# An attention and deformable-convolution block on one core: two of five tile transposes go back to TensorE, and all step orders are new

## The chip, the core and the metric

The kernel runs on one core of a Trainium2 chip. The core has five engines, each with its own instruction queue that is worked off strictly in order: TensorE (PE, matrix products; PEld are its weight loads), VectorE (DVE), ScalarE (ACT), GpSimd (POOL) and SyncE (SP, used here to issue DMAs). Engines wait for each other and for DMAs by semaphores. Data lie in SBUF (128 partitions), matmul results in PSUM, the inputs and scratch arrays in DRAM. The metric is the time of one execution in microseconds; the median of three runs counts.

## What is computed

The input x has 4 images of 64 x 64 pixels with 256 channels, in fp32. Two layers follow each other:

```python
# layer 0: attention over the 4096 pixels of each image
q, k, v = x @ wq + bq, x @ wk + bk, x @ wv + bv            # 32, 32, 256 channels
x = gamma * (softmax(q @ k.T) @ v) + x
# layer 1: DCNv3 block
h = ln(x, ln1_g, ln1_b)
x_proj = h @ inproj_w + inproj_b
x1 = gelu(ln(depthwise_conv3x3(h, dw_w) + dw_b, dwln_g, dwln_b))
offset, mask = x1 @ off_w + off_b, softmax(x1 @ mask_w + mask_b)   # 16 groups, 9 points
out = sum over 9 points of mask * bilinear(x_proj at pixel + point + offset)
x = x + out @ outproj_w + outproj_b
x = x + gelu(ln(x, ln2_g, ln2_b) @ fc1_w + fc1_b) @ fc2_w + fc2_b   # 1024 hidden
```

`ln` normalises a pixel over its 256 channels. Such a normalisation wants the pixels on partitions; the convolution and the matmuls that follow want channels on partitions. So tiles of pixels by channels have to be turned, several times for each pixel.

## The kernel before

**Units.** The work is cut into units of 256 pixels (4 image rows): 16 per image, 64 in all. A unit passes these stages: `project` (queries, keys, values), attention (two units together), `front` (normalisation, input projection), `plan` (depthwise convolution, its normalisation, offsets and masks, sampling weights), `sample` (weighted sum of pixels) and `back` (output projection, MLP). The stages `plan`, `sample` and `back` work on 65 units v = 0 to 64 that are shifted by half a unit, as the convolution needs a row of the next one. Units 0 and 64 have one tile of 128 pixels, the others two.

**Order.** Nothing is ordered by data alone. Each stage is a dictionary of named steps. `whole` (its function is at the end of the kernel) gives each step of each unit a number, sorts all steps by it and emits the instructions in that order; each engine's queue gets its share of this one sequence. The number is `slot * T + WHEN[stage][name]` with T = 120. A slot holds two units, "a" and "b", so the pattern repeats 32 times; `LATE` replaces the numbers in slots at the ends and around a change of image. T is no time: the numbers of `WHEN` lie on a grid of 120/337, that is, they are positions in an order of 337 places per slot. A wait arises where an instruction stands in its queue before what it needs is there.

**Turning a tile.** There are two ways. `transposed` (line 347) makes TensorE transpose 128 x 128 pieces against an identity matrix, four for a tile of 256 x 256, into a PSUM buffer. The other way goes through DRAM: `sent` (line 290) stores the tile to a scratch array `ways`, `blocks` (line 285) loads it back with four DMAs that put its 32 x 32 blocks into their turned places (`in_blocks`, line 70, in runs of 32 numbers, which are 128 bytes), and `swapped` (line 295) turns the insides of the blocks with one VectorE stream transpose of 128 x 512. Before the change five tiles of a unit go through DRAM: the normalised input of `front` (`bl_f`), the convolution of `plan` (`bl_c`), its normalised form (`bl_p`), the sampled sum in `back` (`bl_s`, from `spd`) and the normalised tile before the MLP (`bl_b`). Query, key and value inputs of images 1 to 3 are also loaded in blocks. The first unit and the last ones use TensorE: in `plan` the flag `through` is true for units 1 to 57.

**The steps of `plan` that matter here.** `tap0` (ScalarE) and `tap1` to `tap8` (VectorE) form the convolution `cv`, channels on partitions. `send` stores it (SP queue), `turn` issues the four block loads (SP queue), `swap` makes `pc` with pixels on partitions. `stats` takes mean and variance of pc's rows (VectorE) and starts 1/sqrt on GpSimd, `shift` (VectorE) and `norm` (ScalarE) give `xn`, which `norm` also stores (ScalarE's DMA queue). `turn2` issues four loads again (SP), `swap2` makes `ge`, `gelu` (ScalarE) applies scale, bias and GELU in place. `heads0` and `heads1` (TensorE, 432 columns) give offsets and masks, `bias0` and `bias1` (VectorE) add the biases, and the steps that follow, on VectorE and ScalarE, make sampling weights of them.

**Buffers.** All small products in PSUM (the heads, the hidden layer `ph` in eight pieces, the narrowed `pm`, and those of project, front and back) share the pool tag "m" with two buffers that are taken in turn: the third waits until the first is released. Attention has PSUM buffers of its own (`e0`, `e1`, `acc0`, `acc1`). In SBUF, `xs` (two buffers) holds what `blocks` loads and `cT` (four buffers) the turned tiles; `cv` and `xn` have one buffer each.

Of the kernel before, what the change touches and what calls it, by code (L numbers as in the profile page):

```python
# [20 lines left out]
def tile_attention_dcnv3_block(  # L21
# [23 lines left out]
    nc = tc.nc  # L45
# [301 lines left out]
    def transposed(src, name, n=2, pool=None, tag="m"):  # L347

        pt = (pool or ps).tile([P, C // P, 256], F32, tag=tag, name=f"pt_{name}")
        for k in range(C // P):  # L350
# [19 lines left out]
            "turn": 19.72, "load": 37.2107, "copy": 73.8872, "values": 84.2136, "value_copy": 94.184,  # L370
            "keys": 147.9525, "key_bias": 149.3769,
        },
        "projectb": {
            "turn": 79.72, "load": 112.7003, "copy": 119.822, "values": 126.9436, "keys": 127.6558,
            "value_copy": 130.1484, "key_bias": 132.2849,
        },
        "tablesa": {
            "gelu0": 64.6291, "gelu1": 68.9021, "exp": 84.9258,
        },
        "tablesb": {  # L380
            "gelu0": 158.9911, "gelu1": 170.0297, "exp": 179.2878,
        },
        "fronta": {
            "inverse": -50.3858, "residual": -46.8249, "stats": -45.7567, "shift": -39.7033, "norm": -30.8012,
            "turn": -27.2404, "swap": -12.2849, "scale": -10.1484, "project_in": -5.1632, "image": -4.8071,
            "keep": -4.451, "store": -0.5341, "add": 1.6024,
        },
        "frontb": {
            "inverse": -42.1958, "residual": -41.8398, "stats": -21.8991, "shift": -5.8754, "norm": -0.8902,
            "keep": 9.4362, "turn": 15.1335, "swap": 22.9674, "scale": 27.2404, "image": 29.7329,  # L390
            "project_in": 78.8724, "store": 82.4332, "add": 86.7062,
        },
        "plana": {
            "tap0": -4.095, "tap1": -1.9585, "tap2": 6.2315, "tap3": 8.0119, "tap4": 11.9288, "tap5": 14.7774,
            "tap6": 16.5579, "tap7": 18.3383, "tap8": 19.0504, "send": 23.3234, "turn": 25.1039,
            "carry": 28.3086, "swap": 35.0742, "stats": 37.5668, "shift": 41.8398, "norm": 47.8932,
            "turn2": 51.8101, "swap2": 62.4926, "gelu": 66.4095, "heads0": 70.3264, "bias0": 70.6825,
            "heads1": 71.3947, "bias1": 77.092, "mask_exp": 81.365, "hat0": 82.0772, "hat1": 82.7893,
            "sums": 83.5015, "hat2": 86.3501, "nearer": 87.0623, "invert": 87.4184, "weigh": 89.5549,
            "near": 89.911, "mask": 90.9792, "product0": 92.4036, "y0": 93.1157, "y_copies0": 94.5401,  # L400
            "product1": 95.2522, "y_copies1": 95.9644, "y1": 97.0326, "x_copies": 97.3887, "bounds": 100.5935,
            "x": 101.6617, "count": 105.5786,
        },
        "planb": {
            "tap0": 30.8012, "tap1": 34.7181, "tap2": 38.2789, "tap3": 40.4154, "tap4": 40.7715,
            "tap5": 41.4837, "tap6": 43.6202, "tap7": 45.4006, "tap8": 53.5905, "send": 61.4243,
            "turn": 62.8487, "swap": 68.546, "stats": 69.9703, "shift": 74.5994, "norm": 79.5846,
            "turn2": 88.4866, "carry": 90.6231, "swap2": 98.8131, "gelu": 101.3056, "heads0": 104.1543,
            "heads1": 104.5104, "bias0": 108.0712, "bias1": 108.7834, "mask_exp": 110.2077, "sums": 114.4807,
            "hat0": 116.9733, "hat2": 120.178, "invert": 122.6706, "hat1": 124.095, "nearer": 125.8754,  # L410
            "weigh": 127.2997, "near": 129.0801, "mask": 131.5727, "product0": 140.4748, "y0": 144.3917,
            "y_copies0": 150.4451, "product1": 151.1573, "y_copies1": 152.5816, "y1": 153.2938,
            "x_copies": 153.6499, "x": 156.4985, "count": 186.7656, "bounds": 198.5163,
        },
        "samplea": {
            "rows03": 6.5875, "rows04": 80.6528, "rows14": 83.8576, "rows00": 103.4418, "times00": 103.4421,
            "rows01": 105.9344, "times01": 105.9347, "plus01": 106.2908, "rows02": 106.6466,
            "times02": 106.6469, "times03": 107.003, "plus02": 108.4273, "plus03": 112.3442,
            "times04": 116.6172, "rows12": 117.3291, "times12": 117.3294, "plus04": 118.7537,
            "across00": 122.3145, "rows11": 123.0264, "times11": 123.0267, "across01": 123.3828,  # L420
            "rows13": 128.368, "across02": 133.7092, "rows10": 134.065, "times10": 134.0653,
            "plus11": 136.2018, "plus12": 136.9139, "times13": 141.1869, "times14": 141.543,
            "plus13": 142.6113, "plus14": 143.6795, "across10": 148.6647, "across11": 151.5134,
            "across12": 154.0059,
        },
        "sampleb": {
            "rows04": 135.8457, "rows01": 160.059, "times01": 160.0593, "rows03": 162.1958, "rows02": 162.5516,
            "times02": 162.5519, "rows00": 163.2638, "times00": 163.2641, "plus01": 165.7567,
            "plus02": 168.6053, "times03": 171.454, "plus03": 173.2344, "times04": 176.4392,
            "plus04": 177.5074, "rows13": 178.2196, "across00": 180.0, "across01": 181.7804,  # L430
            "rows11": 183.9166, "times11": 183.9169, "across02": 184.9852, "rows10": 185.3409,
            "times10": 185.3412, "rows12": 186.0531, "times12": 186.0534, "plus11": 187.8338,
            "plus12": 188.1899, "rows14": 191.7507, "times13": 194.9555, "times14": 196.0237,
            "plus13": 201.0089, "plus14": 205.2819, "across10": 211.6914, "across11": 213.4718,
            "across12": 219.1691,
        },
        "backa": {
            "turn": 163.9763, "copy": 166.8249, "load": 171.0979, "project_out": 175.727, "added": 178.9318,
            "stats": 181.0682, "shift": 187.4777, "norm": 192.819, "turn2": 205.638, "swap": 205.9941,
            "scale": 208.1306, "hidden0": 213.8279, "gelu0": 214.8961, "hidden1": 216.6766, "gelu1": 217.7448,  # L440
            "hidden2": 218.457, "gelu2": 220.9496, "hidden4": 222.3739, "hidden6": 222.73, "gelu4": 223.0861,
            "gelu6": 223.7982, "raised": 251.2166, "hidden7": 255.4896, "hidden3": 257.27, "gelu7": 259.4065,
            "gelu3": 259.7626, "hidden5": 264.0356, "gelu5": 264.7478, "narrowed0": 269.0208,
            "narrowed1": 272.2255, "end": 275.7864,
        },
        "backb": {
            "turn": 219.8813, "copy": 230.5638, "load": 233.7685, "project_out": 237.6855, "added": 241.2463,
            "stats": 243.7389, "shift": 250.5045, "norm": 252.6409, "turn2": 260.8309, "swap": 266.5282,
            "raised": 267.5964, "scale": 272.9377, "hidden0": 279.7033, "hidden2": 281.1276, "gelu0": 282.908,
            "hidden7": 284.3323, "gelu2": 284.6884, "hidden5": 286.4688, "gelu7": 287.181, "hidden1": 287.5371,  # L450
            "gelu1": 288.9614, "gelu5": 289.3175, "hidden4": 290.3858, "gelu4": 290.7418, "hidden3": 292.1662,
            "hidden6": 294.3027, "gelu3": 295.0148, "gelu6": 295.3709, "narrowed0": 297.8635,
            "narrowed1": 298.5757, "end": 307.1217,
# [30 lines left out]
        },  # L484
        "attentiona": {
            "load": -59.6439, "k0": -59.2878, "k1": -57.8635, "e0": -55.727, "x0": -48.9614, "e3": -47.8932,
            "x3": -46.4688, "e1": -44.6884, "k2": -44.3323, "x1": -43.2641, "e2": -42.5519, "wa0": -40.7715,
            "x2": -40.0593, "wa1": -38.2789, "e5": -36.8546, "wb0": -35.4303, "k3": -32.2255, "wa2": -29.7329,
            "wb1": -28.6647, "x5": -27.9525, "wb2": -24.3917, "wa3": -23.6795, "e4": -20.4748, "k4": -19.7626,
            "wb3": -17.9822, "x4": -15.1335, "e7": -12.6409, "wb4": -10.8605, "x7": -10.5045, "e6": -8.724,  # L490
            "wa4": -8.0119, "wb5": -6.9436, "x6": -6.5875, "k6": -3.7389, "e9": -1.6024, "wb6": 0.5341,
            "wa5": 0.8902, "x9": 1.9585, "wa6": 4.451, "e8": 4.8071, "x8": 5.5193, "wa7": 8.724, "k5": 9.7923,
            "e12": 10.8605, "wb7": 12.997, "wb8": 13.3531, "x12": 14.4214, "e10": 17.6261, "wb9": 17.9822,
            "x10": 20.1187, "wa8": 21.8991, "e13": 22.2552, "x13": 25.4599, "owna": 26.1721, "wa9": 26.8843,
            "e11": 30.089, "x11": 31.8694, "wb10": 34.362, "wa10": 36.1424, "k7": 36.8546, "wa11": 37.9228,
            "wa12": 38.635, "wa13": 45.0445, "wb11": 48.2493, "e14": 49.6736, "ownb": 52.5223,
# [2495 lines left out]
```

## Time and profile before

| quantity | value |
|---|---|
| median of 3 runs | 3880.85 us (3879.72 to 3881.39) |
| the profiled execution | 3880.23 us |
| its span, from first to last instruction | 3878.4 us |
| granted TensorE clock, mean | 0.983 |
| DMA | 595.09 MB, mean 153 GB/s, 1,024,978 packets, 736,224 of them under 512 B |
| stream transposes for the two tiles of this change | 57 and 57, 0.70 us each |
| transposes by TensorE into pc and for xn of `plan` | 28 and 28 |
| loads bl_c and bl_p | 228 and 228, 64 KB each |
| stores of cv and of plan's xn to ways | 57 and 57, 256 KB each |

Busy time is the time in which an engine executes something, as a share of the span; a queue that waits is not busy. A row of instructions by line gives the line, the engine, what is written and read, shape and count, then the busy time, the mean duration of one in ns, and the idle time just before it with what ended it. Records of TensorE contain the latency of a matmul, so successive ones overlap; what one costs in a full stream is the distance between starts. The chain of waits follows the work back from the last instruction to what released it, step by step.

### The profile page before, as it was taken

The numbers are of one execution on the slowest core, as the hardware profiler recorded it, in microseconds if no ns is written. First come the engines' busy times: TensorE is split into PE (matmuls) and PEld (weight loads), VectorE is DVE, ScalarE is ACT, GpSimd is POOL, SyncE is SP. The second block draws the span as 40 slices with busy tenths as digits, with TensorE's granted clock in tenths as the row PEclk, the third lists the DMA queues.
The fourth block names the chain that finished last, engine by engine and source line by source line (L and its number), as shares of the span: only waits on it lengthen the run. The fifth ranks groups of instructions, "written<-read, shape, count | busy, mean of one in ns | idle before, by whom it ended". The sixth has DMA issues, their size and how long they took to land.

```text
span 3878.4 us, 50276 instructions
## 1 busy us (share of the span) xinstructions
PE 3653.5 (94%) x16106; PEld 3038.3 (78%) x16106; DVE 3588.3 (93%) x5950; ACT 2298.9 (59%) x4300; POOL 789.8 (20%) x702
## 2 busy tenths in 40 slices
PE   7999999999999999999999999999999999998878
PEld 6878888877877878887887888887877778777656
DVE  1289999999999999999999999999999999999995
ACT  3566666555657556665556666655656756676543
POOL 1021221211121221121111122121122122122232
PEclk9999999999999999999999999999999999999989
DMA  5566666776676766676767666676657565644331
GB/s 150 131 147 160 158 169 154 176 182 163 157 180 153 170 161 154 163 176 165 172 162 179 151 160 169 157 175 176 166 140 173 140 160 147 154 131 118 91 97 49
DMA packets 1024978, 595.09 MB, mean 153 GB/s; under 512 B 736224, under 2 KB 937248, under 8 KB 1024704
## 3 DMA queue, kind: packets, MB, share of 16 engines
q1 hardware_dynamic: 930544, 471.09, 51.4%
q10 hardware_dynamic: 92576, 117.23, 10.6%
q0 software_dynamic: 1584, 3.47, 0.3%
q8 instruction: 130, 2.13, 0.2%
q14 instruction: 144, 1.18, 0.1%
HBM read 394.82 MB, written 196.74 MB: 153 GB/s over the span
## 4 chain that ended last, share of the span: by engine, by line
DVE 52%; PE 18%; DMA 14%; issue 7%; SPq 5%; ACT 2%; POOL 1%; DVEq 0%; ACTq 0%; POOLq 0%
DVE pw L2516 12%; DVE pw L2524 9%; DVE cv L2282 9%; PE acc L2160 8%; SPq L76 4%; DVE pr L2427 3%; PE ph L2642 2%; DMA kT<-kd 2%; PE pmlp L2659 2%; DMA bl_s<-spd 2%; DMA ways<-xn_p 2%; PE e L2139 1%; DVE pw L2529 1%; DVE om L2350 1%; DVE hat L2419 1%
## 5 line engine op out<-in xcount | busy, mean ns | idle before, releaser
L2160 PE MATMUL acc<-V,ex 128*128 128x257 f32 x8192 | 1889.5, 381 | 2.9 <-ACT ex L2149 2.8
L2160 PEld LDWEIGHTS acc<-V,ex 128*128 128x128 f32 x8192 | 1558.9, 191 | 241.6 <-issue 5.5
L2516 DVE TENSOR_TENSOR pw<-win,wn 128x1280 f32<-128x1280 f32 x640 | 948.9, 1505 | 15.7 <-DMA win<-xp 10.4
L2524 DVE TENSOR_TENSOR pw<-pw,pw 128x1280 f32<-128x1280 f32 x492 | 751.5, 1527 | 3.7
L2149 ACT ACTIVATE ex<-e 128x512 f32<-128x512 f32 x1024 | 554.1, 592 | 237.8 <-PE e L2139 193.2
L2642 PE MATMUL ph<-hT_b,f1w 128*128 128x256 f32 (+1 forms) x2080 | 522.0, 387 | 73.6 <-ACT gT L2650 28.3
L2282 DVE SCALAR_TENSOR_TENSOR cv<-hs,dw,cv 128x256 f32<-128x256 f32 (+1 forms) x1076 | 529.1, 544 | 2.5 <-ACT cv L2278 2.4
L2642 PEld LDWEIGHTS ph<-hT_b,f1w 128*128 128x128 f32 x2080 | 389.3, 193 | 163.3 <-ACT gT L2650 48.1
L2139 PE MATMUL e<-qs,kT 128*128 128x512 f32 (+1 forms) x1056 | 432.8, 490 | 52.8 <-ACT ex L2149 24.2
L2659 PE MATMUL pmlp<-f2w,gT 128*128 128x256 f32 x2048 | 460.8, 381 | 1.7 <-ACT hT_b L332 1.1
L2650 ACT ACTIVATE gT<-ph,f1b 128x256 f32<-128x256 f32 (+1 forms) x520 | 239.3, 469 | 334.9 <-PE ph L2642 300.8
L2659 PEld LDWEIGHTS pmlp<-f2w,gT 128*128 128x128 f32 x2048 | 390.2, 191 | 58.0 <-ACT hT_b L332 1.4
L2139 PEld LDWEIGHTS e<-qs,kT 128*128 128x128 f32 x1056 | 197.8, 192 | 125.2 <-ACT ex L2149 53.2
L2241 POOL TENSOR_TENSOR xq<-xq,inb 128x512 f32<-128x512 f32 x64 | 141.6, 2212 | 504.8 <-ACT xq L2237 480.7
L2149 ACT ACT_TABLE_LOAD x178 | 228.4, 1283 | 13.4 <-PE e L2139 7.2
L309 POOL TENSOR_SCALAR rstd_p<-mv_p 128x2 f32<-128x2 f32 (+1 forms) x65 | 27.6, 424 | 993.2 <-DVE mv_p L307 968.6
L2341 PE MATMUL po<-om_w,ge 128*128 128x432 f32 x512 | 206.2, 541 | 15.4 <-ACT gT L2650 6.8
L2091 POOL TENSOR_TENSOR x<-x,bv_s 128x512 f32<-128x512 f32 x64 | 118.3, 1864 | 439.1 <-DMA x<-in_x_dram 402.3
L2427 DVE TENSOR_TENSOR pr<-hat 128x1296 f32<-128x1296 f32 x128 | 192.6, 1505 | 0.7
L2341 PEld LDWEIGHTS po<-om_w,ge 128*128 128x128 f32 x512 | 97.1, 195 | 92.0 <-issue 57.5
L2650 ACT ACT_TABLE_LOAD x121 | 155.2, 1283 | 5.2 <-PE ph L2642 2.1
L323 ACT ACTIVATE xn_b<-x1b,nm_b,rstd_b 128x256 f32<-128x256 f32 x128 | 70.0, 593 | 142.7 <-DVE nm_b L315 142.4
(232 smaller groups left out, 4107.3 us busy)
## 6 DMA issues: line engine op xcount, KB each, us to landing
win<-xp SPq DMA_DIRECT2D x536, 320.0 KB, 5.4
kT<-kd ACTq DMA_DIRECT2D x264, 256.0 KB, 3.3
omd<-om SPq DMA_DIRECT2D x63, 432.0 KB, 3.4
x<-in_x_dram SPq DMA_DIRECT2D x64, 256.0 KB, 3.6
x1d<-x SPq DMA_DIRECT2D x64, 256.0 KB, 4.4
xp<-xq SPq DMA_DIRECT2D x128, 128.0 KB, 2.5
spd<-sp SPq DMA_DIRECT2D x63, 256.0 KB, 2.5
x1b<-x1d SPq DMA_DIRECT2D x63, 256.0 KB, 3.1
```

The source lines that it names most:

```text
L76: nc.sync.dma_start(dst[32 * i : 32 * (i + 1)], bass.AP(src.tensor, src.offset + t0 * C + 32 * i, [[C, 32], [P, C // P], [32 * C, 4 * n], ...
L2139: nc.tensor.matmul(e, lhsT=self.kT[t // 4][:, t % 4, :], rhs=q, start=True, stop=not self.general)
L2149: nc.scalar.activation(ex, self.es[r], AF.Exp)
L2160: nc.tensor.matmul(self.acc[u][:, i, :], lhsT=ex[:, i * P : (i + 1) * P], rhs=V[j][:, jj, :], start=(t == 0), stop=(t == NT - 1),)
L2282: nc.vector.scalar_tensor_tensor(dst, src, dw[:, k, j : j + 1], dst, ALU.mult, ALU.add)
L2341: nc.tensor.matmul(st["po", i], lhsT=st["ge"][:, k, i * P : (i + 1) * P], rhs=om_w[:, k, :], start=(k == 0), stop=(k == 1),)
L2427: nc.vector.tensor_mul(pr.rearrange("p a b c d g -> p a b (c d g)"), hat[:, :, i, 1, :].unsqueeze(1).to_broadcast([P, 3, 3, S]), hat[:, :, ...
L2516: nc.vector.tensor_mul(st[i, r].rearrange("p d (g c) -> p (d g) c", c=GC), src.rearrange("p d (g c) -> p (d g) c", c=GC), wns[v][:, i, r] ...
L2524: nc.vector.tensor_add(st[i, 0], st[i, 0], st[i, r])
L2642: nc.tensor.matmul(ph[:, :m], lhsT=f1w[:, k, c * P : (c + 1) * P], rhs=st["hT"][:, k, :m], start=(k == 0), stop=(k == 1),)
L2650: nc.scalar.activation(st["gT"][:, c, :m], st["ph", c][:, :m], AF.Gelu, bias=f1b[:, c : c + 1])
L2659: nc.tensor.matmul(po, lhsT=st["gT"][:, c, i * P : (i + 1) * P], rhs=f2w[:, c, :], start=(c == 0), stop=(c == NH - 1),)
```

## The change

In `plan`, the convolution and its normalised form are turned by TensorE for all units. `turn` issues transposes of `cv` into the PSUM tile `pc`, `turn2` transposes of `xn` into the PSUM tile `pt`; `stats` and `norm` read pc, and `gelu` reads pt, from PSUM. `send`, `swap` and `swap2` are gone with the stores and the loads. `front` and `back` are as before: three tiles of a unit still go through DRAM. The tables `WHEN` and `LATE` are replaced as a whole, so each queue has a new order; a slot has six steps and six places fewer (331).

```diff
-        through = 0 < v < UN - 6 and not general
-
-        def send():
-            st["way"] = sent(2, v, st["cv"], nc.sync)
-
         def turn():
-            if through:
-                st["bl"] = blocks(f"c_{n}", st["way"])
-                return
             st["pc"] = ps.tile([P, 2, C], F32, tag="m", name=f"pc_{n}")
             for i in range(nt):
                 for k in range(C // P):
...
-        def swap():
-            st["pc"] = swapped(p3.tile([P, 2, C], F32, tag="cT", bufs=4, name=f"pc_{n}"), st["bl"])
-
...
         def norm():
             normalised(st, [st["pc"][:, i, :] for i in range(nt)], f"p{n}")
-            if through:
-                st["way2"] = sent(3, v, st["xn"], nc.scalar)
 
         def turn2():
-            if through:
-                st["bl"] = blocks(f"p_{n}", st["way2"])
-            else:
-                st["pt"] = transposed(st["xn"], f"p_{n}", nt)
-
-        def swap2():
-            st["ge"] = swapped(p3.tile([P, C // P, 256], F32, tag="cT", bufs=4, name=f"ge_{n}"), st["bl"])
+            st["pt"] = transposed(st["xn"], f"p_{n}", nt)
 
         def gelu():
-            if through:
-                pt = st["ge"]
-            else:
-                pt = st["pt"]
-                st["ge"] = p3.tile([P, C // P, 256], F32, tag="cT", bufs=4, name=f"ge_{n}")
+            pt = st["pt"]
+            st["ge"] = p3.tile([P, C // P, 256], F32, tag="cT", bufs=4, name=f"ge_{n}")
...
-        if through:
-            d |= {"send": send, "swap": swap, "swap2": swap2}
```

Of the tables, the row of the first unit of a slot in `plan`, up to the heads, as an example:

```diff
         "plana": {
-            "tap0": -4.095, "tap1": -1.9585, "tap2": 6.2315, "tap3": 8.0119, "tap4": 11.9288, "tap5": 14.7774,
-            "tap6": 16.5579, "tap7": 18.3383, "tap8": 19.0504, "send": 23.3234, "turn": 25.1039,
-            "carry": 28.3086, "swap": 35.0742, "stats": 37.5668, "shift": 41.8398, "norm": 47.8932,
-            "turn2": 51.8101, "swap2": 62.4926, "gelu": 66.4095, "heads0": 70.3264, "bias0": 70.6825,
...
+            "tap0": -13.9577, "tap1": -6.7069, "tap2": -3.8066, "tap3": -1.994, "tap4": -0.5438,
+            "tap5": 1.6314, "tap6": 3.8066, "tap7": 9.2447, "tap8": 10.3323, "carry": 13.9577, "turn": 15.7704,
+            "stats": 21.9335, "shift": 29.5468, "norm": 34.2598, "turn2": 44.0483, "gelu": 46.2236,
+            "heads0": 50.2115, "bias0": 51.6616, "heads1": 53.4743, "bias1": 54.5619, "hat0": 54.9245,
...
```

## The prediction

> **What bounds the kernel now.** I read the page's busy shares and slices first, then the chain of waits.
>
> ```profile
> PE 3653.5 (94%) x16106; PEld 3038.3 (78%) x16106; DVE 3588.3 (93%) x5950; ACT 2298.9 (59%) x4300; POOL 789.8 (20%) x702
> ...
> PE   7999999999999999999999999999999999998878
> ...
> DVE  1289999999999999999999999999999999999995
> ...
> DVE 52%; PE 18%; DMA 14%; issue 7%; SPq 5%; ACT 2%; POOL 1%; DVEq 0%; ACTq 0%; POOLq 0%
> ```
>
> Two engines are full from slice 4 to slice 36. The chain runs mostly over VectorE, with 18% on TensorE and 19% on DMAs and SP's queue. To see which of the two sets the pace I cut the trace at the starts of the 64 reciprocals of the attention sums (two per slot of the plan) and asked for busy time per slot. The columns are length, PE, PEld, DVE, ACT, POOL, clock, DMA share, GB/s:
>
> ```profile
> 746.40:865.10 118.70, 111.33 (x489) 92.98 (x488) 112.87 (x184) 68.39 (x130) 23.07 (x20) 0.99 0.72 180
> ...
> 1215.20:1330.20 115.00, 113.83 (x511) 96.30 (x510) 113.58 (x183) 73.16 (x134) 20.51 (x20) 1.00 0.64 152
> 1330.20:1443.50 113.30, 110.49 (x492) 92.32 (x491) 111.87 (x183) 68.36 (x131) 22.96 (x20) 1.00 0.67 162
> 1443.50:1555.90 112.40, 109.35 (x489) 91.83 (x488) 111.78 (x183) 68.37 (x130) 22.14 (x20) 1.00 0.69 163
> ```
>
> In an ordinary slot VectorE is busy 111.8 of 112.4 us: it sets the pace. PE's 109.35 overstates its work, since each record covers the matmul's latency. From start to next start in the trace, a 257-column matmul takes 0.216 us, a 256-column one 0.2155, the 432-column heads 0.3625, the 512-column energies 0.235 (a matmul and two energies after it take 0.686). Per slot that is 256 x 0.216 + 184 x 0.2155 + 16 x 0.3625 + 32 x 0.235 = 55.3 + 39.7 + 5.8 + 7.5 = 108.3 us, 4.1 below the slot. So VectorE is bound, TensorE 3% behind.
>
> Around each change of image some slots are longer (118.7, 117.7, 119.9, 115.0, then 120.2, 116.3, 120.2, 114.4, then 119.0, 117.3): 50 us above an ordinary 112.9. In the first of them VectorE idles 5.8 us. SP's own waits between 746 and 985 us:
>
> ```profile
> SPq L76 <- DMA ways<-cv: 12.3, 4, 6.3
> SPq L76 <- DMA ways<-xn_p: 10.6, 2, 6.4
> ```
>
> SP stands 23 us behind the stores of exactly the two tiles of this change, and every load behind these waits is late.
>
> **The change part by part.** It concerns 57 units (1 to 57); units 0 and 58 to 64 were turned by TensorE already.
>
> *Off VectorE: swap and swap2, 114 stream transposes.* Their rows:
>
> ```profile
> L296 DVE STREAM_TRANSPOSE ge<-bl_p 128x512 f32<-128x512 f32 x57 | 40.2, 705 | 0.8 <-DMA vd<-vs 0.4
> L296 DVE STREAM_TRANSPOSE pc<-bl_c 128x512 f32<-128x512 f32 x57 | 39.9, 700 | 3.0 <-DMA bl_c<-ways 3.0
> ```
>
> 80.1 us in all. In a full slot the durations sum to 124.7 us over 184 instructions that are busy 111.8, so each overlaps its neighbour by 0.07, and one swap is worth 0.63. Four per slot: 2.5 us; VectorE's slot falls from 111.8 to 109.3. stats now reads PSUM: the records of st_p, of both kinds, lie within 392 to 430 ns around 409, so 228 of them cost between 0 and 228 x 0.021 = 5 us; I take 0.
>
> *On TensorE: 4 transposes per tile, 456 in all.* The trace shows them in the last units:
>
> ```profile
> 3441.78 0.60 PE L352 MATMUL pt_f<-ident,xn_f 128*128 128x128 f32 x4
> 3442.22 3.64 PE L2160 MATMUL acc<-V,ex 128*128 128x257 f32 x16
> 3445.69 0.60 PE L2303 MATMUL pc<-ident,cv 128*128 128x128 f32 x4
> 3446.05 0.71 PE L2139 MATMUL e<-qs,kT 128*128 128x512 f32 x2
> ```
>
> Four take 0.44 us from the first start to that of the next matmul, 0.109 each; the weight loads (0.141) keep up. Where the clock was halved (at 3508 us) they stood 0.213 apart. The Trainium skill (TensorE: Matmul & The Clock Gate, Part 4: PE-mode transpose) gives about 275 ns for a transpose in a kernel and says that this mode is not seen as activity by the clock gate. One record here is 273 ns, so figure and record agree, but the next one begins after 109. By the page's figure the sum would be 456 x 0.275 = 125 us, 4.4 per slot: PE would need 112.7 and the change would be worth nothing. By the row it is 456 x 0.109 = 50 us, 1.75 per slot, and PE needs 110.0. I take the row[...].
>
> *Off the queues.* Per unit SP loses one send (0.38) and eight block loads (0.63 each), 5.4 us, ACT's queue one send (0.38). In the 1443 slot the durations of SP's DMA issues sum to 57 us of 112.4, so its capacity isn't the point; what counts is that nothing on SP stands behind `ways<-cv` and `ways<-xn_p`. The DMA engines lose 57 x 2 x 2048 packets of 128 B, 233 thousand of 736 thousand under 512 B; at 0.68 busy that alone gives nothing.
>
> *ScalarE.* Its gelu from PSUM takes 0.556 (pt_p's row) against 0.59 from SBUF, and it is busy 68 of 113 us: nothing either way. Its waits for VectorE's swap2 (128 us in total) become waits for TensorE.
>
> *Two added waits on TensorE.* turn waits for the last tap on VectorE, turn2 for norm on ScalarE. SP, with half its time free, held these waits before; now the accumulating matmuls and the energies queue behind them, ScalarE waits for the energies and VectorE for the heads. Two PSUM buffers (tag "m") serve all small products, 15 per unit before and 17 now, and pc holds one from turn over stats and shift to norm. In the new table these are 18 of 120 parts of a slot for the first unit and 13 for the second; only the narrowed product may share that time. The cost lies between nothing (the order leaves enough between) and the waits before pt_p in the last units of this trace:
>
> ```profile
>   ACT xn_p L323: 9.7, 3
> ```
>
> 9.7 us over 8 units is 1.2 per turn2, and "DVE cv" cost pc 1.5 over 8, 0.2: together 2.8 per slot. Those units run in the drain, where TensorE has little else to do, so I take less: what the slot at 1215 shows, where both engines are near full: PE 112.6 of issue in 115.0, 97.9%, beside VectorE at 98.8%.
>
> *New orders.* Six steps fewer per slot (337 to 331 positions). They can save or lose anywhere; no row shows this. I take nothing.
>
> **The sum.** 294 to 2827 us is 22 slots in 2533 us. PE at 97.9% makes a slot of 110.0/0.979 = 112.4 (VectorE's 109.3 fits with 3 us free): 22 x 112.4 = 2473. Of the 50 us around image changes I leave half, 25, since V and key loads remain there: 2498, or 35 less. From 2827 to 3500 VectorE is bound, with PE mostly at 100 to 108 of 113: 6 slots by 2.5 would be 15 less; half, 7, as new stalls appear. Up to 294 PE alone is bound, and the first units' transposes add 2. After 3500 little changes. -35 - 7 + 2 = -40. The profiled execution took 3880.2 us (span 3878.4, 1.8 around it), 0.6 below the median of the runs, 3880.85: **3840 us**.
>
> **The rivals.**
> 1. *More gain: the stalls at image changes go altogether.* For it: SP's waits above. Against it: kT and V loads are waited for there too, and PE needs 107 to 112 us in these slots. Another 25 less and VectorE's full 15: 3807. Chance 0.10.
> 2. *Gain given back.* PE reaches 96% over all slots, the ordinary ones being 95.9% now (108.3 of 112.9): 110.0/0.96 = 114.6, 22 slots 2521, with 2827 onward as it was: 3870. For it: two engines within 1% of each other; against it: 97.9% was reached once. It lies at the edge of no change. Chance 0.17, 0.09 of it within 0.2%.
> 3. *TensorE takes the place of VectorE and is slower.* Place: turn and turn2, and the product that waits for pc's PSUM buffer. Price: four waits per slot. PE's slack after the change is 112.9 - 110.0 = 2.9, so from 0.7 us per wait on, a slot is longer than before. With the 2.8 of the tail on top of 1.8 of other idle time a slot is 114.6 where it was 112.9, and the long slots stay long: 22 x 1.7 = +37, 3917. For it: the order of TensorE is fixed and the old waits sat on a queue with time to spare; against it: the new table keeps 10 parts between norm and turn2. Chance 0.33.
> That the change doesn't do what it says can be left out: in the compiled order VectorE has 114 stream transposes fewer, TensorE the 456.
>
> **How the numbers follow.** Forecast 0.40, rivals 0.10, 0.17, 0.33. About 0.2% (8 us) can be told from no change. Faster: 0.40 + 0.10 + 0.08 = 0.58, less 0.02 of the forecast's own spread: 0.56. Within 0.2%: 0.09 and 0.02 from the forecast's and the third's edges: 0.11. Slower 0.33. Range 3800 (first rival) to 3920 (third rival at its price); the likeliest case alone 3815 to 3870.
>
> **What would show it.** Right: ordinary slots of 111 to 112.5 us with VectorE under 98% busy and PE issue near 110; no `ways<-cv`; L296 down by 80 us; slots around image changes under 117; the chain's PE share up from 18%. Wrong: PE idle before pc and pt_p of more than 0.7 us each, `ph` or `po` waiting for "DVE nm_p" or ACT xn_p, granted clock below 0.98 in the middle, VectorE's idle moved onto om (for po).

## The result, and the profile after

The changed kernel takes 3892.06 us (median of 11 runs, 3885.96 to 3896.26) where the kernel before takes 3879.11 (11 runs on the same chip): ratio 1.0034, 95% interval 1.0025 to 1.0043. That is 13 us slower, and 52 us above the forecast. The profiled execution's span is 3891.9 us, 13.5 above that of before.

The page of the changed kernel, parts 1 and 2 (the chain of waits is cut short in this trace, its shares sum to 21%, so it isn't read):

```profile
PE 3686.7 (95%) x16562; PEld 3089.4 (79%) x16562; DVE 3544.5 (91%) x5836; ACT 2316.4 (60%) x4322; POOL 870.0 (22%) x702
...
PE   7999999999998999999998999999999999998878
...
DVE  1289999999989999999998999999999999999995
```

TensorE has its 456 transposes more, VectorE its 114 instructions less and 44 us less of busy time, not the 72 (114 by 0.63) that were forecast. One number was not looked at in the prediction: GpSimd makes the same 702 instructions and is busy 870.0 us where it was 789.8.

The slots (cut as before, at the reciprocals of the attention sums) tell where. Ordinary ones of the changed kernel, with the same columns as before:

```profile
641.40:756.70 115.30, 111.52 (x501) 93.57 (x500) 112.16 (x179) 69.32 (x131) 27.04 (x20) 0.99 0.57 139
...
2381.50:2496.70 115.20, 111.42 (x498) 93.47 (x497) 112.12 (x179) 69.30 (x132) 26.84 (x20) 0.99 0.57 141
2496.70:2612.10 115.40, 112.32 (x505) 94.73 (x504) 112.13 (x179) 70.31 (x133) 25.36 (x20) 0.99 0.57 141
```

A slot has 179 VectorE instructions instead of 183, yet these are busy 112.1 us, as 183 were (111.8). And it is 115.3 us long (114.2 to 115.4 among the ordinary slots but one of 116.7), so VectorE now idles 3.2 us, where it idled 0.6. Four instructions are gone and no time with them: the others have become longer.

Which ones, summed by tile over three slots of each kernel: `pc` and `ge` (the swaps) take 2.57 us less per slot. Against it `nm_p` takes 1.34 more (139 to 804 ns each), `pw<-win,wn` and `pr` 1.07 each, `us` 0.90, two more groups of `pw` 0.75 and 0.52, `mk` 0.64; `cv` and `wn` take 2.72 and 1.08 less. An instruction whose tiles are 128x2 cannot have become longer by its own work. The timeline around one of them, GpSimd first and VectorE under it (columns: start, us, engine, line, operation, tiles, shapes, count, idle before and its releaser):

```profile
2442.75 1.36 POOL L309 TENSOR_SCALAR rstd_p<-mv_p 128x2 f32<-128x2 f32 x1 [12.38 <-DVE mv_p L307]
2444.19 1.82 POOL L310 TENSOR_TENSOR rstd_p<-rstd_p,minus_half 128x2 f32<-128x2 f32 x1
2445.99 2.00 POOL L2629 TENSOR_TENSOR x1b<-x1b,f2b 128x512 f32<-128x512 f32 x1
2447.95 2.52 POOL L2252 TENSOR_TENSOR x<-x,ob 128x512 f32<-128x512 f32 x1
2452.39 1.43 POOL L2120 TENSOR_TENSOR x<-x,bv_s 128x512 f32<-128x512 f32 x1 [1.93 <-DMA x<-in_x_dram]
```

```profile
2445.37 3.96 DVE L2521 TENSOR_TENSOR pw<-win,wn 128x1280 f32<-128x1280 f32 x2
2449.26 1.37 DVE L2451 TENSOR_TENSOR us<-pr 128x144 f32<-128x144 f32 x1
2450.55 0.30 DVE L2452 TENSOR_TENSOR us<-pr 128x144 f32<-128x144 f32 x1
...
2452.61 1.23 DVE L315 SCALAR_TENSOR_TENSOR nm_p<-mv_p,rstd_p 128x2 f32<-128x2 f32 x1
2453.76 0.87 DVE L2311 SCALAR_TENSOR_TENSOR cv<-hs,dw,cv 128x256 f32<-128x256 f32 x2
```

Three adds of GpSimd, three VectorE instructions too long by 1.1 us: the second `pw` (2.56 instead of 1.48; the pair reads 3.96), the first `us` (1.37, its twins 0.30), and `nm_p` (1.23 for 128x2). Each begins while an add runs and ends as if its own work had begun only at the add's end. It holds the other way too: `rstd_p`, two numbers per partition, takes 1.36 and 1.82 us behind a `pw`, 0.22 and 0.71 where it starts alone. The Trainium skill has the rule that the prediction missed (SBUF — State Buffer, section "SBUF: two separate sides"): VectorE and GpSimd share a pair of SBUF ports, which one of them holds for a whole instruction, and one of the cases in which a VectorE instruction contends for it is that it has two SBUF inputs and the GpSimd one reads SBUF. The trace agrees, and adds the price: up to 1.1 us per 128x512 add.

Now the kernel before, around one of its adds, GpSimd and then VectorE:

```profile
2294.99 2.93 POOL L2241 TENSOR_TENSOR xq<-xq,inb 128x512 f32<-128x512 f32 x1 [17.06 <-ACT xq L2237]
```

```profile
2295.30 1.48 DVE L2524 TENSOR_TENSOR pw<-pw,pw 128x1280 f32<-128x1280 f32 x1
2296.70 0.70 DVE L2010 STREAM_TRANSPOSE xT<-xs 128x512 f32<-128x512 f32 x1
2297.33 0.65 DVE L2615 TENSOR_TENSOR x1b<-x1b,pout 128x512 f32<-128x512 f32 x1
```

The add waits for `pw`, then runs beside a stream transpose (one input) and an addition from PSUM (one SBUF input), and both keep their usual 0.70 and 0.65. Here the add costs VectorE nothing. Counted over three slots (what an instruction took beyond its undisturbed time while a GpSimd add ran), the eight adds of a slot cost VectorE 5.6 us before and 7.95 after. By add that is 0.7 us before and 1.0 after. Were the removed transposes the cover that is now missing? Hardly: in the 22 slots before, the adds last 305.6 us in all, and the removed transposes lie beside them for 6.3 us (ten of `ge`, none of `pc`). What covered the adds in the three slots were mostly `xT`'s transposes, the additions of `pout`, the statistics `st_b` and the reduction `ms`. These are all still there; the new order put the adds beside other work.

The greater part of the 3.2 us of idle is a wait for GpSimd, too. From the groups by line of the changed kernel (columns as in the page's part 5):

```profile
L315 DVE SCALAR_TENSOR_TENSOR nm_p<-mv_p,rstd_p 128x2 f32<-128x2 f32 (+1 forms) x65 | 42.6, 656 | 2.5 <-POOL rstd_p L310 2.5
...
L315 DVE SCALAR_TENSOR_TENSOR nm_f<-mv_f,rstd_f 128x2 f32<-128x2 f32 x64 | 20.4, 318 | 24.5 <-POOL rstd_f L310 24.5
L315 DVE SCALAR_TENSOR_TENSOR nm_b<-mv_b,rstd_b 128x2 f32<-128x2 f32 (+1 forms) x65 | 15.9, 244 | 19.4 <-POOL rstd_b L310 19.4
```

Before, these three waited 2.4, 2.9 and 3.1 us. Now `nm_f` and `nm_b` wait 44 us for GpSimd's `rstd`, in an ordinary slot 1.1 and 0.9 us, once each. One such wait of `nm_f`, GpSimd and then VectorE:

```profile
2383.55 0.22 POOL L309 TENSOR_SCALAR rstd_f<-mv_f 128x2 f32<-128x2 f32 x1 [6.43 <-DVE mv_f L307]
2383.85 0.71 POOL L310 TENSOR_TENSOR rstd_f<-rstd_f,minus_half 128x2 f32<-128x2 f32 x1
```

```profile
2383.16 0.30 DVE L307 BATCH_NORM_AGGREGATE mv_f<-st_f 128x2 f32<-128x6 f32 x2
2384.59 0.16 DVE L315 SCALAR_TENSOR_TENSOR nm_f<-mv_f,rstd_f 128x2 f32<-128x2 f32 x1 [1.13 <-POOL rstd_f L310]
```

GpSimd is not late here: it starts at once and takes its shortest times, 0.22 and 0.71 us. The new order puts `nm_f` directly behind `mv_f` on VectorE, so VectorE stands for the whole way over GpSimd; in the three slots of before it starts 1.1 us after the end of `rstd_f` in one unit of a slot and 14.4 us in the other. In front of `nm_b` there is one `pw`, behind which `rstd_b`'s first part takes 1.36 us. No add of 128x512 takes part in either.

So an ordinary slot: 112.6, less 2.6 for the swaps, plus 2.3 of lengthened instructions, plus 2.6 of new idle (2.0 of it for `rstd`, the rest for `kq` and `ms` on ScalarE), gives 114.9; measured 115.2. Over the execution: start -3.1, the 22 slots up to 2827 us +17.8, the next stretch (to 3620 us) -4.0, the end +2.8.

### The profile page after: what moved, and what is told of

It is laid out like the page before. It is cut to its first block, busy times and chain, and to the rows that moved or that the text cites. A ratio compares the mean times of both kernels' runs of the same rounds, so it can differ in the third digit from the quotient of the medians.

```text
span 3891.9 us, 50082 instructions
## 1 busy us (share of the span) xinstructions
PE 3686.7 (95%) x16562; PEld 3089.4 (79%) x16562; DVE 3544.5 (91%) x5836; ACT 2316.4 (60%) x4322; POOL 870.0 (22%) x702
## 5 line engine op out<-in xcount | busy, mean ns | idle before, releaser
L2189 PE MATMUL acc<-V,ex 128*128 128x257 f32 x8192 | 1916.8, 383 | 0.9 <-ACT ex L2178 0.6
L2521 DVE TENSOR_TENSOR pw<-win,wn 128x1280 f32<-128x1280 f32 x640 | 970.8, 1532 | 7.4 <-PE sum L2554 2.9
L2311 DVE SCALAR_TENSOR_TENSOR cv<-hs,dw,cv 128x256 f32<-128x256 f32 (+1 forms) x1076 | 453.9, 470 | 5.1 <-ACT cv L2307 5.0
L2168 PE MATMUL e<-qs,kT 128*128 128x512 f32 (+1 forms) x1056 | 420.1, 480 | 4.1 <-ACT ex L2178 4.1
L309 POOL TENSOR_SCALAR rstd_b<-mv_b 128x2 f32<-128x2 f32 (+1 forms) x65 | 60.5, 931 | 1156.7 <-DVE mv_b L307 1156.7
L2434 DVE TENSOR_TENSOR pr<-hat 128x1296 f32<-128x1296 f32 x128 | 215.3, 1682 | 0.9 <-ACT us L2449 0.3
L2270 POOL TENSOR_TENSOR xq<-xq,inb 128x512 f32<-128x512 f32 x64 | 108.4, 1694 | 374.8 <-ACT xq L2266 360.1
L309 POOL TENSOR_SCALAR rstd_p<-mv_p 128x2 f32<-128x2 f32 (+1 forms) x65 | 56.4, 868 | 579.3 <-DVE mv_p L307 576.7
L2375 ACT ACTIVATE hat<-om 128x576 f32<-128x576 f32 (+1 forms) x130 | 87.3, 673 | 145.7 <-DVE om L2357 143.9
L309 POOL TENSOR_SCALAR rstd_f<-mv_f 128x2 f32<-128x2 f32 x64 | 45.6, 712 | 512.0 <-DVE mv_f L307 507.6
```

What stands on the lines that cost most here:

```text
L309: nc.gpsimd.tensor_scalar(r[:, :n], mv[:, :n, 1], EPS, None, ALU.add)
L2168: nc.tensor.matmul(e, lhsT=self.kT[t // 4][:, t % 4, :], rhs=q, start=True, stop=not self.general)
L2189: nc.tensor.matmul(self.acc[u][:, i, :], lhsT=ex[:, i * P : (i + 1) * P], rhs=V[j][:, jj, :], start=(t == 0), stop=(t == NT - 1),)
L2311: nc.vector.scalar_tensor_tensor(dst, src, dw[:, k, j : j + 1], dst, ALU.mult, ALU.add)
L2434: nc.vector.tensor_mul(pr.rearrange("p a b c d g -> p a b (c d g)"), hat[:, :, i, 1, :].unsqueeze(1).to_broadcast([P, 3, 3, S]), hat[:, :, ...
L2521: nc.vector.tensor_mul(st[i, r].rearrange("p d (g c) -> p (d g) c", c=GC), src.rearrange("p d (g c) -> p (d g) c", c=GC), wns[v][:, i, r] ...
```

## The experiments

Ratios are against the kernel before on the same chip, with 95% intervals.

**1. GpSimd's adds taken away, in both kernels.** The four adds (`constant`, `keep`, `add`, `raised`) are cut to one channel of 256, so 255 channels stay without these biases.

```diff
-nc.gpsimd.tensor_tensor(xq, xq, inb.unsqueeze(1).to_broadcast([P, 2, C]), ALU.add)
+nc.gpsimd.tensor_tensor(xq[:, :, :1], xq[:, :, :1], inb[:, :1].unsqueeze(1).to_broadcast([P, 2, 1]), ALU.add)
```

> The kernel before, with GpSimd's four 128x512 bias adds (constant, keep, add, raised) cut to one channel of each tile, so 255 of 256 bias channels are left out; every wait and the order stay. Port theory (a GpSimd add holds up one VectorE instruction with two SBUF inputs by about 1.0 us; 5.6 us per slot in the trace before): VectorE busy per ordinary slot 111.8 -> about 106.2, TensorE with 108.3 us of issue becomes the bound, ordinary slots 109 to 111.5 us, 3780 to 3835 us in all. Rival (the stretched VectorE instructions have another cause, such as DMA writes): VectorE stays at 111 to 112 us per slot and the time within 10 us of 3879.

> The changed kernel with the same four GpSimd adds cut to one channel (255 of 256 bias channels left out). Port theory (the changed kernel lost its 2.5 us per slot to 2.3 us more of GpSimd stretching and 2.0 us of VectorE waiting for GpSimd's rstd): VectorE busy per ordinary slot 112.2 -> about 104.3, the waits of nm_f and nm_b shrink under 0.3 us each, TensorE with 110.0 becomes the bound, slots 110.5 to 112.5 instead of 115, 3800 to 3845 us. Rival (TensorE's new waits set the pace: turn, turn2, the hidden layer waiting for added to release its PSUM buffer): ordinary slots stay above 114 and the time above 3870, with ph still idle for 3 to 5 us per slot.

Measured: before 3731.42 us (0.9605, 0.9589 to 0.9621), changed 3731.2 (0.9615, 0.9599 to 0.9631). Both lie below their ranges: the gains are larger than expected, and without the adds the two kernels tie. The adds cost the kernel before 150 us and the changed one 161, a difference of 11 where the change lost 13. An ordinary slot of the kernel before, then one of the changed kernel:

```profile
505.70:614.80 109.10, 108.53 (x488) 92.11 (x487) 106.71 (x184) 67.76 (x130) 13.23 (x20) 1.00 0.70 168
```

```profile
614.80:725.10 110.30, 110.30 (x506) 93.72 (x505) 104.79 (x180) 70.43 (x132) 16.48 (x20) 1.00 0.60 147
```

VectorE's busy time falls from 112.0 to 106.7 in the one and from 112.1 to 104.8 in the other: with the adds the change frees nothing on VectorE, without them 1.9 us. So the lengthening comes from the adds. The waits for `rstd` don't: they were expected to shrink under 0.3 us each, and stay as they were in the whole execution,

```profile
DVE nm_f L315 <- POOL rstd_f L310: 24.5, 22, 1.2
DVE nm_b L315 <- POOL rstd_b L310: 19.4, 22, 1.0
```

but cost nothing here, where VectorE has time to spare. The hidden layer's wait on TensorE (`ph`, 1.7 to 3.7 us in ordinary slots of the changed kernel) is gone, so it followed from VectorE's lateness. And why does the changed kernel not win here, with 1.9 us less on VectorE? Because VectorE waits for TensorE; one of these waits, in the whole execution:

```profile
DVE rall L2216 <- PE acc L2189: 70.5, 22, 26.6
```

It waits 1.0 us per ordinary slot for TensorE's accumulating matmuls (9 such waits with the adds, 22 without). TensorE never stands in such a slot, which takes 110.3 us against the 110.0 of issue that were forecast. In the kernel before, the slots away from an image change take 108.0 to 112.3 us, 109.9 in the mean, where 108.3 of issue were worked out. TensorE sets the pace of both, or nearly, and what the transposes add to it is not seen in the total.

**2. Two of the four adds moved to TensorE, in both kernels.** The biases of output projection and second MLP layer are added in PSUM by one fp32r matmul (64 rows) per 256-column product; `keep`'s add and `raised` go.

```diff
+                biasing(po[:, i, :], ob)
...
-            nc.gpsimd.tensor_tensor(att.x[u], att.x[u], ob.unsqueeze(1).to_broadcast([P, 2, C]), ALU.add)
```

> The kernel before, with two of the four GpSimd adds gone for good: the output projection's bias and the second MLP bias are added in PSUM by one more matmul each (fp32r, 256 columns, 0.109 us by its columns; 4 per unit, 0.87 us of TensorE per slot). Port theory: these two adds stretch VectorE by 4.1 us per slot in the trace before, so VectorE 111.8 -> 107.7, TensorE 108.3 -> 109.2, ordinary slots 110 to 112, 3800 to 3855 us. Rival (no port contention): TensorE longer by 0.9, VectorE as before, 3875 to 3905 us.

> The changed kernel with the same two biases moved into PSUM. Port theory: keep and raised stretch VectorE by about 5 us per slot in the changed kernel; VectorE 112.2 -> 107 to 108, TensorE 110.0 -> 110.9, so TensorE is bound: slots 111.5 to 113.5, 3820 to 3865 us, no better than the kernel before with the same edit. Rival (TensorE's waits set the pace): 3880 to 3910 us.

Measured: before 3844.71 (0.9904, 0.9888 to 0.9921), changed 3861.37 (0.9948, 0.9931 to 0.9964). Both gain and both times lie in their ranges, though by luck, for the slots are longer than forecast (mostly over 113 us in the kernel before, 114.3 in the changed one); the changed kernel is the slower. Its slot of 114.3 has VectorE busy 107.7 and TensorE all the time: TensorE is the bound. A bias matmul cost far more than the 0.109 us I had put down: from `pmlp`'s last start to the bias 0.309 instead of 0.2155, and from there to the next matmul 0.309 to 0.312, so 0.40 each and 3.2 us per slot.

**3. All four adds given to VectorE itself, in both kernels.** For the projection VectorE evicts PSUM and adds at once, in place of ScalarE's eviction; `keep` and `constant` change as `raised` does.

```diff
 def store():
-    nc.scalar.copy(st["xq"], st["pp"])
+    nc.vector.tensor_tensor(st["xq"], st["pp"], inb.unsqueeze(1).to_broadcast([P, 2, C]), ALU.add)
 def add():
-    nc.gpsimd.tensor_tensor(xq, xq, inb.unsqueeze(1).to_broadcast([P, 2, C]), ALU.add)
...
-    nc.gpsimd.tensor_tensor(x1n, x1n, f2b.unsqueeze(1).to_broadcast([P, n, C]), ALU.add)
+    nc.vector.tensor_tensor(x1n, x1n, f2b.unsqueeze(1).to_broadcast([P, n, C]), ALU.add)
```

> The changed kernel with GpSimd's four kinds of 128x512 add given to VectorE: x+bv_s, x+ob and x1b+f2b as they stand, and the projection's bias added while VectorE itself evicts PSUM (pp+inb), in place of ScalarE's eviction and GpSimd's add. Theory (GpSimd's adds hold up VectorE's two-input instructions, and in the changed kernel more than before): the 7.95 us of stretched instructions in an ordinary slot go, eight adds of about 0.63 us come (x1b<-x1b,pout measures 0.65), and the waits for rstd shrink: VectorE 109.3 busy, slot 111 to 112, 3795 us (3770 to 3830). Rival (the changed kernel lost its gain to waits around TensorE, and VectorE stays the bound): eight adds of 0.63 us are simply added, 5 us a slot, 28 slots: about 4030 us.

> The kernel before with the same edit. Theory: 5.6 us of stretched instructions go and 5.0 us of adds come, so a slot is shorter by 0.6 us: 3862 us (3845 to 3885), some 70 us above the changed kernel with the same edit. Rival: 5 us a slot are added, about 4020 us, and the changed kernel with this edit is not faster than this one.

Measured: changed 3827.56 us (0.987, 0.9853 to 0.9886), before 3940.45 (1.0168, 1.0149 to 1.0187). More work on the engine that sets the pace makes the changed kernel 64 us faster. Two slots of it:

```profile
513.80:625.60 111.80, 110.77 (x507) 93.65 (x505) 108.89 (x188) 69.72 (x132) 12.40 (x12) 1.00 0.58 144
1534.50:1646.30 111.80, 110.77 (x507) 93.69 (x505) 108.89 (x188) 69.73 (x131) 12.40 (x12) 1.00 0.59 145
```

Eight instructions more than 179 (the window's edge cuts one more), and 108.9 busy instead of 112.1. No VectorE instruction is lengthened by an add any more. The waits for `rstd` didn't shrink here either (26.1 and 18.8 us), though no add is left on GpSimd. The kernel before missed its range (3845 to 3885): VectorE's busy time came out as worked out (111.3), but the slot grew to 119, as VectorE stood 92 us in all for the load of `x`, whose add it now makes itself. That run therefore doesn't compare the kernels fairly; number 5 takes this add out of the edit.

**4. Only the projection's add moved, in both kernels** (the first two edits of number 3).

> The changed kernel with only the projection's bias moved (VectorE evicts pp+inb; ScalarE's eviction and GpSimd's add go). Theory: two of the eight adds held up VectorE by about 1 us each, two instructions of 0.65 us come: 0.6 us less a slot, 3873 us (3850 to 3890). Rival: 1.3 us more a slot, 3928 us.

> The kernel before with only the projection's bias moved. Theory: these two adds lay partly beside single-input work and stretched VectorE by only some 0.7 us together, and 1.3 us come: 0.6 us more a slot, 3896 us (3875 to 3915), so the edit helps the changed kernel and hurts the one before. Rival: 1.3 us more a slot, 3915 us.

Measured: changed 3876.56 (1.0001, 0.9992 to 1.0010), 15 us faster than without the edit; before 3904.8 (1.0072, 1.0055 to 1.0088), 28 us slower. Same edit, opposite signs: in the changed kernel these two adds met two-input instructions, in the kernel before they lay partly beside single-input ones. VectorE's busy time per slot went from 112.1 to 111.1 in the one and from 112.0 to 112.5 in the other. The kernel before lost more than 0.6 us a slot, since VectorE also came to wait for the loads `bl_b`, 2.2 us a slot.

**5. Three adds to VectorE, `constant` left with GpSimd, in both kernels.**

> The kernel before with three of the four adds given to VectorE (pp+inb, x+ob, x1b+f2b); x+bv_s stays with GpSimd, since VectorE stood 92 us for this x's load when it made that add too. Theory: VectorE 111.2 to 111.8 busy in an ordinary slot against 112.0 before, so no gain is to be had: 3875 to 3915 us, and the changed kernel with the same edit lies at least 40 us below it. Rival (the change frees no time of VectorE): both within 15 us of each other.

> The changed kernel with the same three adds given to VectorE, x+bv_s left with GpSimd. Theory: of 7.95 us of stretched instructions in an ordinary slot only the 1.7 us of x+bv_s stay, six adds of 0.63 us come: VectorE 109.6 to 110, slot 112 to 113, 3838 us (3825 to 3855). Rival: as for the kernel before, no gain of it, 3885 or more.

Measured: before 3866.65 (0.9975, 0.9968 to 0.9982), changed 3832.63 (0.9888, 0.9871 to 0.9904). One slot of the kernel before with this edit, and one of the changed kernel:

```profile
1440.70:1554.40 113.70, 110.17 (x490) 91.91 (x489) 110.78 (x189) 67.11 (x128) 11.35 (x14) 1.00 0.65 162
```

```profile
1541.90:1654.20 112.30, 111.04 (x505) 93.51 (x504) 109.36 (x185) 69.76 (x131) 15.98 (x14) 1.00 0.59 145
```

With this edit the change is worth 34 us, where it costs 13 with GpSimd's adds in place. That is less than the 40 that were expected, since the kernel before gained where it was expected to stay (3875 to 3915); the rival's 15 is far off. But the 34 don't measure the freed time alone: with this edit the VectorE of the kernel before waits 53 us for the loads `bl_b` over the whole execution, where it waited 20 without. What the change frees is seen in VectorE's busy time, 109.4 against 110.8 us per slot.

**6. The image change.** At two of its three changes of image the changed kernel stands still; VectorE's and TensorE's waits in the slot at 1091 us:

```profile
DVE hT_f L296 <- DMA bl_f<-ways: 12.4, 1, 12.4
```

```profile
PE pc L2324 <- DVE cv L2311: 11.9, 1, 11.9
```

The swap of `hT_f` waits for its block loads, and `pc`, now on TensorE's queue, waits for the convolution behind it. There the swap, the scaling and the image's copy were moved 11 units later in the front's `LATE` table, in the changed kernel and in that of number 3; one of three such places:

```diff
-                "norm": -34.27078, "turn": -29.46441, "keep": -24.31473, "swap": -21.56823, "scale": -18.13511,
-                "image": -12.2988, "project_in": 3.49355, "store": 16.1961, "add": 32.33177,
+                "norm": -34.27078, "turn": -29.46441, "keep": -24.31473, "swap": -10.56823, "scale": -7.13511,
+                "image": -1.29880, "project_in": 3.49355, "store": 16.1961, "add": 32.33177,
```

> The changed kernel with one thing moved: at the image changes VectorE's swap of hT_f, its scaling and the image's copy stand 11 units (about 11 us of the plan) later in the order. Theory of the image changes (the new order put this swap only 8 units behind the issue of its block loads instead of 16, and VectorE stood 11 to 12 us at two of them, TensorE behind it at pc): most of the two waits goes, 15 to 24 us less: 3872 us (3862 to 3882), and VectorE's wait for bl_f falls from 27 us to under 8. Rival (the wait only moves on to the convolution's first tap, cv, that needs this image): no gain, 3885 to 3900. The theory of GpSimd's adds says nothing of it: ordinary slots stay at 115.

> The changed kernel with both edits: VectorE makes the four adds, and the swap at the image changes stands 11 units later. If both causes are separate their gains add: 3828 less 10 to 20, 3812 us (3803 to 3822). Rival: the wait only moves on, 3825 to 3832.

Measured: 3885.62 us (1.0024, 1.0015 to 1.0033) and 3823.39 (0.9865, 0.9849 to 0.9882). Either is 4 to 6 us below its kernel without the edit, and the intervals overlap. The first lies in the rival's range, the second between the forecast's and the rival's. The waits for `bl_f` fell from 27.4 to 9.4 us in all (under 8 was expected), so most of this time was lost again elsewhere. In the slot at 1091 of the first, VectorE's wait for `bl_f` is 2.4 us and TensorE's is still

```profile
PE pc L2324 <- DVE cv L2311: 7.4, 1, 7.4
```

3823.39 us is the fastest of the kernels that compute everything, 1.35% below before; number 3's 3827.56 can't be told from it. Turning the two tiles on TensorE with the order of before, which would part the transposes from the new order, wasn't tried: there `pc` would hold one of the two PSUM buffers of tag "m" across products that need both. Nor was `nm_f` moved away from `mv_f`, which would price the waits for `rstd`.

## Why the prediction was wrong

The step that failed is *"VectorE's slot falls from 111.8 to 109.3"*, and under it the term *"New orders. … I take nothing"*, set to nothing because no row showed it. The removed work was sized rightly (2.5 us forecast, 2.57 measured), but the rest was taken to stay as long as it was and to follow without new waits. Both depend on what stands beside and before what in the new order, and GpSimd has no line in the prediction. The runs put in its place: VectorE still busy 112.1 us, as lengthening by GpSimd's adds rose from 5.6 to 7.95 us per slot, and 2.6 us of new waits, 2.0 of them for `rstd`.

None of these 4.9 us per slot comes from the transposes' own cost. That the adds cause the lengthening is shown by number 1. That the new order brought adds and two-input instructions together, and not the swaps' absence, is read from the trace (6.3 of 305.6 us of cover); no run has one without the other. What the waits for `rstd` cost in time, no run shows either.

In number 5 the changed kernel has slots of 112.3 us and VectorE busy 109.4, close to the sum's 112.4 and 109.3. That is chance: six adds are on VectorE there, and the waits for `rstd` remain.

**TensorE's 50 us** held. The new transposes start 0.109 us apart, and where nothing else is in the way (number 1) a slot takes 110.3 us for the 110.0 forecast. So the row was right, and not the sum made with the 275 ns of the page. The granted clock is 0.99 between 400 and 3500 us in both kernels, so the new transposes didn't lower it.

**Rival 3** named the right sign with the wrong mechanism, and its slot of 114.6 lies near the measured one by chance. TensorE's waits in ordinary slots, 1.7 to 3.7 us, are nearly all for `x1b` on VectorE, and go when VectorE is on time. Only at the image changes does TensorE stand for long in front of `pc`, 11.9 and 10.4 us at two of them.

**"Half of the 50 us around image changes".** Against five ordinary slots of their own kernel, the five from 746 us on were 20.3 us longer before (583.8 against 563.5), and the five from 752 us on are 10.2 longer now (586.2 against 576.0). Half it was, but on top of longer slots, and not for the reason given: what VectorE waits for longest there is `bl_f`, not V or the keys.

**Of the signs listed**, no `ways<-cv`, L296 down by 80 us, VectorE under 98% and TensorE's 110 came true; slots of 111 to 112.5, and those around image changes under 117, didn't. Of the signs of being wrong none came in an ordinary slot: TensorE doesn't stand before `pc` or `pt_p`, and `ph` waits for `x1b`. The list had none for GpSimd.

## What to carry to other kernels

Before you take work from VectorE or change its order, list GpSimd's instructions and look at what VectorE does beside each: a single-input instruction, or one that reads PSUM, may be the cover under which GpSimd works for nothing, and a new order can put two-input instructions in its place. Look also at short ways over another engine, such as `mv`, `rstd`, `nm`: if nothing stands between, VectorE waits for all of it. If an elementwise add on GpSimd holds up VectorE for longer than VectorE would need for it (in the changed kernel 1.0 to 1.1 us against 0.65), try to give it back. That depends on the order: in the kernel before, where the adds cost 0.7 us each, the edit of number 3 lost 64 us and that of number 4 28, partly in new waits for loads, and that of number 5 gained 10. And ask, before freeing the engine that sets the pace, how far below it the next one lies: here TensorE's 110.3 us left 2.3 of a slot of 112.6 to be won at most.

## What the runs showed of the hardware that was not expected

- A GpSimd add of 128x512 (1.26 to 1.45 us alone) lengthened a two-input VectorE instruction behind its start by up to 1.1 us, whatever the size: 0.15 to 1.23 at 128x2, 0.30 to 1.37 at 128x144, 1.48 to 2.56 at 128x1280. Stream transposes and additions from PSUM beside an add kept their 0.70 and 0.65.
- GpSimd's smallest instructions pay as well: the first of `rstd` (128x2) took 1.36 us behind a VectorE product of 128x1280, and 0.22 alone.
- A 64-row fp32r matmul of 256 columns between fp32 ones cost 0.40 us: 0.31 of its own and 0.09 at the matmul before it, against 0.2155 for a full fp32 one. Whether the rows or the type do it wasn't tried.
